# Loading 28 of the gathered edge chunks row by row from two other engines in a graph attention kernel

## The chip, the cores and the metric

The kernel runs on one core of a Trainium2 chip. The metric is the device time of one execution in microseconds (us); lower is better. TensorE is PE in the profile, VectorE DVE, ScalarE ACT, GpSimd POOL, SyncE SP. "SPq" and "ACTq" are records of an engine's instruction queue, such as the issue of a DMA.

## What is computed

One layer of graph attention with 4 heads of 32 over 12,500 nodes and 200,000 edges sorted by target, added to its input. Cut to what matters:

```
h = relu(layernorm(x))                         # node features, 128 wide
hn = (h @ W_node.T).reshape(N, 4, 32)
e = (edge_features @ W_edge.T).reshape(E, 4, 32)
att = sum(concat([hn[src], hn[tgt], e]) * a)   # one logit per edge and head
att = where(att > 0, att, 0.2 * att)
m = maximum(segment_max(att, tgt), 0)
ex = exp(att - m[tgt])
denom = segment_sum(ex, tgt) + (E - deg) * exp(-m)
out = x + segment_sum(ex / denom[tgt] * hn[src], tgt)
```

`hn[src]` reads one row of a node table per edge: a random read of 200,000 rows.

## The kernel before

A first part (about 90 us) normalizes the nodes and writes `table` to DRAM: one row of 137 floats (548 bytes) per node, with the projected features and the source part of the logits. Edges stand in groups of 512 places (511 edges and a first place that takes over a sum from the group before); a group has J = 4 chunks of 128, one edge per partition. QG = 4 groups are a quad; there are nq = 98 quads, q = 0 to 97. Supers are mostly 4 quads (near the ends 2 or 3); the softmax runs once per super.

For each quad `gather(q, ...)` issues 16 indirect DMAs on GpSimd (L183), one per chunk; each fetches 128 rows of `table` by the indices in `srci` into `ga`, a ring of QUADS = 8 quads. `open_logits(q)` orders the gathers of quad q + 2, so that GpSimd works through the quads in order, and a ring place must be free of the quad eight before it.

`all_logits(q)` makes the logits of a quad on TensorE (L686, L689) from edge features `ea`, one-hot target matrices `at` (VectorE, L656, from `db`), and target weights `pw`; SyncE loads these. In the next quad's logits `add_sources(q)` lets ScalarE wait until all 16 gathers of the quad have landed, and copies the source logits out of `ga` into `U` (L733). This copy is called U(q) below. At a super's end `softmax` goes through ScalarE, VectorE and TensorE in turn (on ScalarE low L795, low L800, fac L857, stack L869, xs L887).

`sums(q)` runs about five quads behind: per group, VectorE weighs the gathered rows (L1067 or L1026) and makes a one-hot matrix (L1069 or L1009), TensorE sums (L1100). Up to quad 74 several groups share one accumulation; from quad 75 on each group is its own, and between two groups ScalarE copies a carried row into the next group (ga L919) and a finished sum out (pt L979), with a TensorE product (L911) between the two; at a quad's end ScalarE makes `den` (L985). Each of the four steps of `sums(q)` is interleaved with a step of the logits of a later quad; instructions of one engine run in the order written.

`db_all` holds two tiles of target places of 4 x 512 integers for each partition; from quad 10 on only a quarter of each is used (bytes instead of integers).

Of the kernel before, what the change touches and what calls it, by code (L numbers as in the profile page):

```python
# [9 lines left out]
F32 = mybir.dt.float32  # L10
# [4 lines left out]
OP = mybir.AluOpType  # L15
AX = mybir.AxisListType

P = 128
# [8 lines left out]
R_CNT, R_SRC, ROW = H * HW, H * HW + 1, H * HW + 5  # L27

J = 4
GE = J * P  # L30
NE = GE - 1
WIDE, NARROW = 112, 80
QG = 4
# [13 lines left out]
SQUARE = 32  # L47
TWO = 2
HELD = 3
SETS = max(NODE_T, QG * J)  # L50
PAD = 1 << 20


def blocks(total, step):
    return [(i, min(step, total - i)) for i in range(0, total, step)]
# [14 lines left out]
def kernel(  # L70
# [39 lines left out]
    nc = tc.nc  # L110
    NT = -(-(N + P) // P)
    NP = NT * P
# [8 lines left out]
    table = dram.tile([NP, ROW], F32, name="table")  # L121
# [33 lines left out]
    quads = blocks(G, QG)  # L155
    nq = len(quads)
    first_fold = nq - FOLDS
# [6 lines left out]

    spare = consts.tile([P, 6 * SBG * H], F32, name="spare")
    ga_all = consts.tile([P, QUADS, QG, J, ROW], F32, name="ga")
    GA, GATHERED = {}, set()
    arrived = [tc.alloc_semaphore(f"rows{k}") for k in range(QUADS)]
    landings = {}

    def gather(q, rows, width, lo, hi):

        g0, m = quads[q]
        ga = GA[q] = ga_all[:, q % QUADS]
        chunks = lambda i: -(-min(E - (g0 + i) * NE + 1, GE) // P)
        for i in range(lo, hi):
            if chunks(i) < J:
                nc.vector.memset(ga[:, i, chunks(i):, :], 0.0)
        order = [(i, j) for i in range(lo, hi) for j in range(chunks(i))]
        if q >= 2 * QUADS:  # L180
            order.sort(key=lambda at: at != (hi - 1, 0))
        for i, j in order:
            came = nc.gpsimd.indirect_dma_start(  # L183
                out=ga[:, i, j, 0:width], out_offset=None, in_=rows,
                in_offset=bass.IndirectOffsetOnAxis(ap=srci[:, g0 + i, j:j + 1], axis=0))
            if q >= QUADS:
                came.then_inc(arrived[q % len(arrived)], 16)
                tc.no_tile_sem_insts.add(came.ins.name)
                tc.add_to_no_dep_group(f"rows{q}", came.ins)
                landings[q] = landings.get(q, 0) + 16  # L190
# [27 lines left out]
    with tc.manual_schedule():  # L218
# [4 lines left out]
        for m in sorted({m for _, m in supers}):  # L223
            for p in range(-(-m // 2)):
                n = min(2, m - 2 * p) * QG
                to = of_head[m, p] = consts.tile([PAIR * KH, H * m * QG], F32, name=f"of_head{m}_{p}")
# [17 lines left out]
        for _ in range(AT_ONCE):  # L244
            q, i = early.pop(0)
# [129 lines left out]
        db_all = stay.tile([P, 2, QG, GE], I32, name="db")  # L375
# [20 lines left out]
        with tc.tile_pool(name="node", bufs=2) as node, tc.tile_pool(  # L396
# [117 lines left out]
            for b, (t0, T) in enumerate(sets):  # L514
# [5 lines left out]
                row = node.tile([P, NODE_T, ROW], F32, name="row")  # L520
# [24 lines left out]
    with tc.tile_pool(name="work", bufs=2) as work, \  # L545
# [34 lines left out]
        def windows(of, size, w, n):  # L580
# [5 lines left out]
        as_bytes = lambda d: d.bitcast(U8)  # L586
        rows_at = lambda d, at, size, n: as_bytes(d.rearrange("n c -> (n c)"))[
            bass.ds(at, n * size)].rearrange("(n c) -> n c", c=size)
# [44 lines left out]
        def fetch_rows(s):  # L633
            g0, m = groups(s)
            dr = DR[s] = turned.tile([SBG * H, NE + 2], I32, name="dr", bufs=2)
            if finer(s) > 1:
# [4 lines left out]
            nc.sync.dma_start(dr[0:H * m, :],  # L641
                              dst_rows[g0:g0 + m, :].unsqueeze(0).to_broadcast([H, m, NE + 2]))

        def open_logits(q):
            if q == supers[of_quad[q]][0]:
                fetch_rows(of_quad[q])
            if q + 2 < nq:
                fetch(q + 2)
            AT[q] = work.tile([P, QG, GE], BF16, name="at")
# [68 lines left out]
        def add_sources(q):  # L718

            s = of_quad[q]  # L720
            g0, m = quads[q]
            s0, sm = groups(s)
            keep_logits(q)
            if s not in U:
                U[s] = turned.tile([P, J, SBG * H], F32, name="U", bufs=2)
            f = finer(s)
            u = U[s][:, 0:J // f, 0:sm * H * f].rearrange("p c (h w) -> p w c h", h=H)[
                :, (g0 - s0) * f:(g0 - s0 + m) * f]
            if q >= QUADS:
                nc.scalar.wait_ge(arrived[q % len(arrived)],  # L730
                                  sum(landings[a] for a in range(QUADS, q + 1)
                                      if a % len(arrived) == q % len(arrived)))
            taken = nc.scalar.copy(u, GA[q][:, :m].rearrange("p g (f c) r -> p (g f) c r", f=f)[  # L733
                :, :, :, R_SRC:R_SRC + H])
            if q >= QUADS:
                tc.declare_no_dep(taken.ins, group=f"rows{q}",
                                  reason="a semaphore counts the gathers of this quad")
                tc.declare_fence(taken.ins, group=f"rows{q}")
            for kept in (EA, DB, PW, AT):
                del kept[q]  # L740
# [153 lines left out]
        state = {"step": 0}  # L894

        def complete(window=True, all_due=False):

            state["step"] += 1
            division = None
            if divisions and "hold" not in state and (  # L900
                    all_due or divisions[0][-1] is None or divisions[0][-1] + 2 <= state["step"]):
                division = divisions.pop(0)
            if begun and window:
                complete_window(*begun.pop())
            if division:
                divide(*division)
# [132 lines left out]
        def sums(q):  # L1039
# [8 lines left out]
            s = of_quad[q]  # L1048
# [3 lines left out]
            k, span = class_of(q)  # L1052
# [23 lines left out]
            for i in range(m):  # L1076
                g = g0 + i
                if first_fold - 4 <= q < first_fold - 4 + FOLDS:
                    shifts(q + 4, i)
                on_gpsimd = early and (q, i) > (first_fold - 2, QG - 2)  # L1080
                if (q, i) not in AHEAD:
                    weighed(nc.gpsimd if on_gpsimd else nc.vector, ga, i,
                            heads(XE[s] if on_gpsimd else ex)[:, :, :, g - s0])
                    if not early:
                        mark(q, i, hot)
                new = i % k == 0
                if not i and not later:
                    entered()
                    settled()
                if new:  # L1090
                    second = k == 2 and i > 0
                    if not second:
                        bank = ps.tile([P, 512], F32, name="acc", bufs=3)
                    acc = bank[0:1 + span, ROW:2 * ROW] if second else bank[0:1 + span, 0:ROW]
                    fc = fac if g == s0 else None
                if later and i == m - 1:
                    entered()
                least_j = 1 if k == 1 else 0
                for j in range(least_j, J)[::-1]:
                    nc.tensor.matmul(acc, hot[:, i, j, 0:1 + span], ga[:, i, j, :],  # L1100
                                     start=new and j == J - 1 and not second,
                                     stop=k > 1 and i % k == k - 1 and j == least_j,
                                     skip_group_check=k > 1)
                if i == (2 if later else 1):
                    passed_on(fac if g0 == s0 else None)
                    if later:
                        settled()
                if not later and i == (2 if k > 1 else 1):
                    entered()
                    if k == 1:  # L1110
                        settled()
                complete(new)
                if k == 1:
                    begun.append((q, i, ga, hot, pt, acc, fc))
                if i == 2 and QUADS <= q < first_fold - 5 and of_quad[q + 1] == s:
                    READY[q + 1] = marks(q + 1)
                    beside_rows(q + 1)
                    RESTED.add(q + 1)
                if k > 1 and i == m - 1:
                    state["pending"] = q, bank  # L1120
                if QUADS <= q < first_fold - 5:
                    if i % TWO == 0 and (q, i + 1) not in AHEAD and i + 1 < m:
                        weighed(nc.vector, ga, i + 1, heads(ex)[:, :, :, g + 1 - s0])
                        mark(q, i + 1, hot)
                        AHEAD.add((q, i + 1))
                    elif i % TWO and i + 1 < m:
                        ready(q, i + 1, ga, hot)
                    elif i + 1 == m and q + 1 in READY:
                        ready(q + 1, 0, GA[q + 1], READY[q + 1])
                issue("inputs", "results")  # L1130
                yield
# [417 lines left out]
        with tc.manual_schedule():  # L1549
# [20 lines left out]
            for s, (q0, m) in enumerate(supers):  # L1570
# [17 lines left out]
                for k in range(m if s == 1 else m - 1):  # L1588
                    now, ahead = ahead[:1], ahead[1:]
                    several_sums = [sums(q0 + k)]  # L1590
                    if s == len(supers) - 3:
                        held_sums = sums(q0 + k + 1)
                        several_sums.append(islice(held_sums, HELD))
                    early_marks = (marked(first_fold - 2, first_fold - 1)
# [235 lines left out]
```

## Time and profile before

| | |
|---|---|
| median of 3 runs | 1998.37 us (1998.31 to 1999.74) |
| the profiled execution | 2000.29 us, span 1998.4 us |
| PE busy | 57% |
| DVE busy | 60% |
| ACT busy | 16% |
| POOL busy | 75% |
| mean granted TensorE clock | 0.732 |

The time of the profiled execution is 1.9 us above its span. In the lists, a group of instructions has its line, engine, operation, output and inputs, count, then busy time and mean ns of one, then the idle time of the engine just before and what ended it. A row of the timeline has start, duration, engine, line, operation, count, and in brackets the idle time before it. A row of waits has who waited for what, us in total, times, and the longest. Issuing a DMA is not counted as busy time of its engine.

### The profile page before, as it was taken

The numbers are of one execution on the slowest core, as the hardware profiler recorded it, in microseconds if no ns is written. First come the engines' busy times: TensorE is split into PE (matmuls) and PEld (weight loads), VectorE is DVE, ScalarE is ACT, GpSimd is POOL, SyncE is SP. The second block draws the span as 40 slices with busy tenths as digits, with TensorE's granted clock in tenths as the row PEclk, the third lists the DMA queues.
The fourth block names the chain that finished last, engine by engine and source line by source line (L and its number), as shares of the span: only waits on it lengthen the run. The fifth ranks groups of instructions, "written<-read, shape, count | busy, mean of one in ns | idle before, by whom it ended". The sixth has DMA issues, their size and how long they took to land. (4 is left out here: it accounts for less than half of the span.)

```text
span 1998.4 us, 18710 instructions
## 1 busy us (share of the span) xinstructions
PE 1145.4 (57%) x5116; PEld 779.1 (39%) x5116; DVE 1195.9 (60%) x2695; ACT 320.7 (16%) x1077; POOL 1496.4 (75%) x1596
## 2 busy tenths in 40 slices
PE   6566676555464555564646555646464554465565
PEld 5444354334243333343434333434343333234344
DVE  8676787456365554563755646637556465468585
ACT  6564111001001010010010100100101011122122
POOL 7777777777777777777777777777777777777775
PEclk9788788677676776766767767667677677777777
DMA  7754754434344434444444444444443453445441
GB/s 253 208 134 99 174 135 115 101 97 112 95 111 101 119 98 109 101 109 111 115 104 120 98 116 103 110 111 116 103 117 94 106 123 95 123 98 123 101 98 42
DMA packets 167746, 229.56 MB, mean 115 GB/s; under 512 B 60827, under 2 KB 100669, under 8 KB 167638
## 3 DMA queue, kind: packets, MB, share of 16 engines
q0 software_dynamic: 50112, 109.61, 24.9%
q1 hardware_dynamic: 115824, 116.14, 20.3%
q10 hardware_dynamic: 1702, 2.59, 0.4%
q8 instruction: 41, 0.67, 0.1%
q14 instruction: 67, 0.55, 0.1%
HBM read 210.74 MB, written 17.43 MB: 114 GB/s over the span
## 5 line engine op out<-in xcount | busy, mean ns | idle before, releaser
L183 POOL DMA_INDIRECT ga<-table,srci x1494 | 1413.2, 946 | 456.6 <-issue 427.1
L1100 PE MATMUL acc<-ga,hot 128*113 128x137 f32 (+1 forms) x2928 | 544.7, 346 | 95.3 <-DVE hot L1009 55.2
L1100 PEld LDWEIGHTS acc<-ga,hot 128*113 128x113 f32 (+1 forms) x2928 | 484.5, 215 | 193.4 <-issue 80.2
L947 DVE SCALAR_TENSOR_TENSOR pt<-pt,spare,acc 1x133 f32<-1x133 f32 x113 | 38.3, 339 | 517.9 <-ACT den_of L941 516.5
L689 PE MATMUL lg<-at,pw 112*96 112x512 bf16 (+2 forms) x392 | 156.4, 435 | 271.7 <-DVE at L656 257.5
L686 PE MATMUL lg<-ea,by_pair 128*96 128x512 f32 (+1 forms) x392 | 230.8, 674 | 11.4 <-ACT tg L699 11.4
L656 DVE TENSOR_TENSOR at<-const_ps,db 112x1024 bf16<-112x1024 f32 (+1 forms) x176 | 212.7, 1209 | 5.0 <-DMA db<-offset 4.1
L1067 DVE TENSOR_TENSOR ga<-ga,ex_ps 128x1056 f32<-128x1056 f32 x147 | 182.3, 1240 | 0.0
L790 PE MATMUL t_ps<-ident,U 128*64 128x128 f32 (+2 forms) x210 | 46.6, 393 | 196.5 <-ACT U L733 196.5
L733 ACT COPY U<-ga 128x64 f32<-128x64 f32 x98 | 29.0, 298 | 756.4 <-DMA ga<-table,srci 756.1
L1069 DVE TENSOR_TENSOR hot<-const_ps,slot 128x896 f32<-128x896 f32 (+1 forms) x147 | 144.2, 981 | 0.0
L881 PE MATMUL ex_ps<-ident,stack 128*128 128x128 f32 x105 | 28.8, 427 | 188.8 <-DVE stack L871 176.2
L790 PEld LDWEIGHTS t_ps<-ident,U 128*64 128x64 f32 (+2 forms) x210 | 37.1, 200 | 221.7 <-ACT U L733 216.1
L881 PEld LDWEIGHTS ex_ps<-ident,stack 128*128 128x128 f32 x105 | 18.6, 215 | 202.9 <-ACT stack L869 202.9
L689 PEld LDWEIGHTS <-pw 112*96 112x96 bf16 (+2 forms) x392 | 54.4, 139 | 104.4 <-issue 101.9
L966 PEld LDWEIGHTS acc<-pt,spare 1*2 1x2 f32 x226 | 14.0, 86 | 207.9 <-issue 199.6
L183 POOL DMA_INDIRECT ga<-in_x_dram,srci x72 | 68.3, 949 | 23.3 <-issue 18.9
L1026 DVE TENSOR_TENSOR ga<-ga,ex_ps 128x528 f32<-128x528 f32 x92 | 63.5, 693 | 36.5 <-ACT xs L887 36.5
L699 ACT COPY tg<-lg 96x512 f32<-96x512 f32 (+1 forms) x51 | 29.6, 580 | 291.9 <-PE lg L689 275.0
L715 PE MATMUL t_ps<-tg,of_head 96*64 96x512 f32 (+3 forms) x96 | 71.0, 831 | 3.4 <-ACT tg L699 3.4
L715 PEld LDWEIGHTS t_ps<-tg,of_head 96*64 96x64 f32 (+3 forms) x96 | 11.8, 170 | 153.0 <-issue 146.8
L686 PEld LDWEIGHTS lg<-ea,by_pair 128*96 128x96 f32 (+1 forms) x392 | 63.7, 188 | 18.2 <-ACT tg L699 13.8
(205 smaller groups left out, 1314.0 us busy)
## 6 DMA issues: line engine op xcount, KB each, us to landing
ea<-in_edge_t_dram SPq DMA_DIRECT2D x196, 256.0 KB
ga<-table,srci POOLq DMA_INDIRECT x1494
db<-offset SPq DMA_DIRECT2D x53, 256.0 KB
db<-in_dst_dram SPq DMA_DIRECT2D x20, 320.0 KB
db<-offset SPq DMA_DIRECT2D x35, 160.0 KB
table<-row SPq DMA_DIRECT2D x9, 616.5 KB
xt<-in_x_dram SPq DMA_DIRECT2D x9, 576.0 KB
inputs<-in_x_dram SPq DMA_DIRECT2D x92, 56.0 KB
```

What stands on the lines that cost most here:

```text
L183: came = nc.gpsimd.indirect_dma_start(out=ga[:, i, j, 0:width], out_offset=None, in_=rows, in_offset=bass.IndirectOffsetOnAxis(ap=srci[:, ...
L656: nc.vector.tensor_tensor(AT[q][:span, i:i + n, :].rearrange("p g e -> p (g e)"), part_ps[:span].to_broadcast([span, n * GE]), DB[q][:span ...
L686: nc.tensor.matmul(lg, by_pair[:, begin:begin + n], ea[:, i // 2, :], start=half == 0 and i == 0, stop=False, skip_group_check=True)
L689: nc.tensor.matmul(lg, PW[q][:span, begin:begin + n], at[:span, i, :], start=False, stop=full and i == quads[q][1] - 1, skip_group_check=True)
L715: nc.tensor.matmul(TP[s][:groups(s)[1] * H], of_head[supers[s][1], p][:n], tg[:n], start=p == 0, stop=False, skip_group_check=True)
L790: nc.tensor.matmul(t_ps[:R, j * P:(j + 1) * P], u[:, j, :R], ident, start=False, stop=j == C - 1, skip_group_check=True)
L881: nc.tensor.transpose(turned_ps[:, j, :], stack[:, j * P:(j + 1) * P], ident)
L947: nc.vector.scalar_tensor_tensor(to, row(w + at), passing[:, w + at:w + at + 1], own, op0=OP.mult, op1=OP.add)
L1026: engine.tensor_tensor(val, val, weight.unsqueeze(3).to_broadcast([P, J, H, HW]), op=OP.mult)
L1067: nc.vector.tensor_tensor(val, val, weight.unsqueeze(3).to_broadcast([P, TWO * J, H, HW]), op=OP.mult)
L1069: nc.vector.tensor_tensor(hot[:, i:i + TWO, :, 1:1 + span].rearrange("p g j c -> p (g j) c"), lane_ps[:, 0:span].unsqueeze(1).to_broadcast ...
L1100: nc.tensor.matmul(acc, hot[:, i, j, 0:1 + span], ga[:, i, j, :], start=new and j == J - 1 and not second, stop=k > 1 and i % k == k - 1 a ...
```

## The change

28 chunks are no longer gathered on GpSimd. In each of the four steps of `sums(q)`, for q = 12 to 91, ScalarE issues 7 loads of one table row each and SyncE 5, into tiles of their own in the unused part of `db_all` (two tiles for each of the engines). 19 steps of ScalarE fill one chunk (16 chunks in all, each the last chunk of a quad's last group), 26 steps of SyncE another (12 chunks, the chunk before that). The row addresses come from the index list: a DMA fetches 128 indices onto one partition, VectorE multiplies them by the row's bytes, and every fourth step the engine loads 28 (or 20) of them into registers. Each row counts on a semaphore; before U(q) ScalarE waits for the 128 rows of the chunk and copies them into the ring.

```
 SINGLES_FROM = 12
...
-        order = [(i, j) for i in range(lo, hi) for j in range(chunks(i))]
+        order = [(i, j) for i in range(lo, hi) for j in range(chunks(i)) if (q, i, j) not in SINGLE]
...
+        class Singles:
+            def __init__(self, engine, kind, some, j, at):
+                self.engine, self.kind, self.some, self.j = engine, kind, some, j
+                free = db_all.rearrange("p k g e -> p k (g e)")[:, :, GE * (1 + at):GE * (2 + at)]
+                self.rows = [free[:, k, 0:ROW].bitcast(F32) for k in range(2)]
+                self.places = [free[0:1, k, 2 * P:3 * P] for k in range(2)]
+                self.semaphores = [nc.alloc_semaphore(f"single{at}_{k}") for k in range(3)]
+                self.steps = -(-P // some)
+                self.step, self.first, self.count = 0, None, {}
+            def target(self, n):
+                return self.first + n * self.steps // QG
+            def chunk(self, n):
+                return self.target(n), QG - 1, self.j
+            def fetch_places(self, n):
...
+                self.engine.dma_start(self.places[n % 2], src[at:at + P].unsqueeze(0))
+            def scale_places(self, n):
+                if self.target(n) < nq - 2:
+                    nc.vector.tensor_scalar(self.places[n % 2], self.places[n % 2], float(4 * ROW),
+                                            None, op0=OP.mult)
+            def advance(self):
+                if self.first is None:
+                    self.first = state["opened"] + -(-self.steps // QG) + 1
+                    self.fetch_places(0)
+                    self.scale_places(0)
+                n, at = divmod(self.step, self.steps)
+                self.step += 1
+                q, i, j = self.chunk(n)
+                if q >= nq - 2:
+                    return
+                if not at:
+                    SINGLE[q, i, j] = self, n
+                    self.fetch_places(n + 1)
+                if at == QG // 2:
+                    self.scale_places(n + 1)
+                lo = at * self.some
+                if at % QG == 0:
+                    upto = min(lo + QG * self.some, P)
+                    self.values = nc.values_load_multi_w_load_instructions(
+                        self.places[n % 2][:, lo:upto], engines=[self.kind], ...)[1]
+                for p in range(lo, min(lo + self.some, P)):
+                    came = self.engine.dma_start(
+                        as_bytes(self.rows[n % 2][p:p + 1, :]),
+                        rows_at(table, self.values[p - at // QG * QG * self.some], 4 * ROW, 1))
+                    came.then_inc(self.semaphores[n % 3], 16)
...
+            def put(self, n, to):
+                nc.scalar.wait_ge(self.semaphores[n % 3], 16 * P * (n // 3 + 1))
+                taken = nc.scalar.copy(to, self.rows[n % 2])
...
+        SINGLES = [Singles(*of, at) for at, of in enumerate([(nc.scalar, mybir.EngineType.Activation, 7, 3), (nc.sync, mybir.EngineType.SP, 5, 2)])]
...
 def open_logits(q):
+            state["opened"] = q
...
 def add_sources(q):
+            for (a, i, j), (of, n) in list(SINGLE.items()):
+                if a == q:
+                    of.put(n, GA[q][:, i, j, :])
+                    del SINGLE[a, i, j]
...
 def sums(q):
                 complete(new)
+                if SINGLES_FROM <= q < first_fold - 5:
+                    for of in SINGLES:
+                        of.advance()
```

With first = opened + ceil(steps / 4) + 1 the n-th chunk of ScalarE belongs to quad 22 + 19n/4 (rounded down), that of SyncE to quad 24 + 26n/4. ScalarE's last rows are issued in `sums(87)`, SyncE's in `sums(89)`.

ScalarE, from U(84) to U(85), in the part where each group is its own accumulation. Before (U is L733, the carried row L919, the finished sum L979, the one-hot column and the softmax columns of the next quad L998 and L1037, den L985):

```order
L733 COPY U<-ga 128x4x16
L919 COPY ga<-acc 1x133
L979 COPY pt<-acc 81x137
L998 CAST hot<-is_last 128x16
L1037 COPY ga<-xs 128x16x5
L919 COPY ga<-acc 1x133
L979 COPY pt<-acc 81x137
L919 COPY ga<-acc 1x133
L979 COPY pt<-acc 81x137
L985 ACTIVATE den<-pt 81x16
```

After, the same beginning (lines are 80 higher; `DMA db<-table` are the row loads, `TENSOR_LOAD db` loads 28 addresses into registers):

```order
L813 COPY U<-ga 128x4x16
L999 COPY ga<-acc 1x133
L1059 COPY pt<-acc 81x137
L695 TENSOR_LOAD db
L700 DMA db<-table 1x548 x7
L1078 CAST hot<-is_last 128x16
L1117 COPY ga<-xs 128x16x5
L999 COPY ga<-acc 1x133
L1059 COPY pt<-acc 81x137
L700 DMA db<-table 1x548 x7
L999 COPY ga<-acc 1x133
L1059 COPY pt<-acc 81x137
```

Seven loads now stand behind each finished sum, ahead of the next carried row.

ScalarE in a softmax quad, from U(86). Before:

```order
L733 COPY U<-ga 128x4x16
L919 COPY ga<-acc 1x133
L979 COPY pt<-acc 81x137
L795 ACTIVATE low<-t_ps 64x511
L919 COPY ga<-acc 1x133
L979 COPY pt<-acc 81x137
L800 COPY low<-t_ps 64x511
L919 COPY ga<-acc 1x133
L979 COPY pt<-acc 81x137
L857 ACTIVATE fac<-fac 1x4
```

After:

```order
L700 DMA db<-table 1x548 x7
L875 ACTIVATE low<-t_ps 64x511
L999 COPY ga<-acc 1x133
L1059 COPY pt<-acc 81x137
L695 TENSOR_LOAD db
L700 DMA db<-table 1x548 x7
L880 COPY low<-t_ps 64x511
L999 COPY ga<-acc 1x133
L1059 COPY pt<-acc 81x137
L700 DMA db<-table 1x548 x7
L937 ACTIVATE fac<-fac 1x4
```

A block of loads stands ahead of each of the first three softmax steps. Two more blocks follow behind den of that quad (L985 before, L1065 now), ahead of the next U.

SyncE, a quad of the middle part (out: results; inputs: rows of x for the sum; ea, db, pw: for the logits). Before:

```order
L596 DMA out_dram<-res 112x512
L596 DMA ea<-in_edge_t_dram 128x512
L596 DMA out_dram<-res 112x512
L582 TENSOR_LOAD base_row
L596 DMA inputs<-in_x_dram 112x512
L582 TENSOR_LOAD base_side
L596 DMA inputs<-in_x_dram 112x512
L596 DMA pw<-side 112x24
```

After:

```order
L597 DMA out_dram<-res 112x512
L597 DMA ea<-in_edge_t_dram 128x512
L700 DMA db<-table 1x548 x5
L597 DMA out_dram<-res 112x512
L583 TENSOR_LOAD base_row
L700 DMA db<-table 1x548 x5
L597 DMA inputs<-in_x_dram 112x512
L583 TENSOR_LOAD base_side
L700 DMA db<-table 1x548 x5
L597 DMA inputs<-in_x_dram 112x512
L597 DMA pw<-side 112x24
```

Five loads stand between SyncE's other transfers, four times a quad.

More of the change, by code (lines that the diff above doesn't have):

```diff
@@ L49 @@
 HELD = 3
+SINGLES_FROM = 12
 SETS = max(NODE_T, QG * J)
@@ L166 @@
     ga_all = consts.tile([P, QUADS, QG, J, ROW], F32, name="ga")
-    GA, GATHERED = {}, set()
+    GA, GATHERED, SINGLE = {}, set(), {}
     arrived = [tc.alloc_semaphore(f"rows{k}") for k in range(QUADS)]
@@ L642, in fetch_rows @@
                               dst_rows[g0:g0 + m, :].unsqueeze(0).to_broadcast([H, m, NE + 2]))
+        class Singles:
[15 more added lines that the diff above has]
+                    return
+                g = quads[q][0] + i
+                at = ((g // 2 * J + j) * 2 + g % 2) * P
+                self.engine.dma_start(self.places[n % 2], src[at:at + P].unsqueeze(0))
[10 more added lines that the diff above has]
+                self.step += 1
+                q, i, j = self.chunk(n)
+                if q >= nq - 2:
+                    return
+                if not at:
+                    assert q not in GATHERED
+                    SINGLE[q, i, j] = self, n
[6 more added lines that the diff above has]
+                    self.values = nc.values_load_multi_w_load_instructions(
+                        self.places[n % 2][:, lo:upto], engines=[self.kind], min_val=0,
+                        max_val=(NP - 1) * 4 * ROW,
+                        skip_runtime_bounds_check_because="a node's row")[1]
+                for p in range(lo, min(lo + self.some, P)):
[3 more added lines that the diff above has]
+                    came.then_inc(self.semaphores[n % 3], 16)
+                    tc.no_tile_sem_insts.add(came.ins.name)
+                    tc.add_to_no_dep_group(f"single{self.j}_{n}", came.ins)
+                    self.count[n] = self.count.get(n, 0) + 1
+            def put(self, n, to):
+                assert self.count[n] == P
+                nc.scalar.wait_ge(self.semaphores[n % 3], 16 * P * (n // 3 + 1))
+                taken = nc.scalar.copy(to, self.rows[n % 2])
+                tc.declare_no_dep(taken.ins, group=f"single{self.j}_{n}",
+                                  reason="a semaphore counts the rows of this chunk")
+                tc.declare_fence(taken.ins, group=f"single{self.j}_{n}")
```

## The prediction

> **What bounds the kernel now.** I read the page's engine table and groups first, then the waits, then ScalarE's timeline.
>
> ```profile
> PE 1145.4 (57%) x5116; PEld 779.1 (39%) x5116; DVE 1195.9 (60%) x2695; ACT 320.7 (16%) x1077; POOL 1496.4 (75%) x1596
> L183 POOL DMA_INDIRECT ga<-table,srci x1494 | 1413.2, 946 | 456.6 <-issue 427.1
> ```
>
> GpSimd is the busiest engine, and its idle time is almost all "issue": it waits for nothing between two gathers.
>
> ```profile
> ACT U L733 <- DMA ga<-table,srci: 756.1, 73, 19.4
> POOL ga L183 <- issue: 446.0, 1463, 0.6
> ```
>
> In the list of waits the gather line has 1463 pauses of 0.3 us mean (446.0/1463) and none over 0.6, so GpSimd never stops for anyone; ScalarE stands 756 us at the copy U, which needs the quad's gathered rows. I write U(q) for the copy of quad q, and count them back from the last, q = 97. ScalarE's timeline shows where that wait has room:
>
> ```profile
> 1006.14 0.30 ACT L733 COPY U<-ga 128x64 f32<-128x64 f32 x1 [19.34 <-DMA ga<-table,srci]
> 1026.13 0.30 ACT L733 COPY U<-ga 128x64 f32<-128x64 f32 x1 [11.34 <-DMA ga<-table,srci]
> 1046.13 0.30 ACT L733 COPY U<-ga 128x64 f32<-128x64 f32 x1 [0.90 <-DMA ga<-table,srci]
> 1066.03 0.30 ACT L733 COPY U<-ga 128x64 f32<-128x64 f32 x1 [9.01 <-DMA ga<-table,srci]
> 1086.03 0.30 ACT L733 COPY U<-ga 128x64 f32<-128x64 f32 x1 [19.35 <-DMA ga<-table,srci]
> ...
> 1585.64 0.30 ACT L733 COPY U<-ga 128x64 f32<-128x64 f32 x1 [11.63 <-DMA ga<-table,srci]
> 1613.74 0.30 ACT L733 COPY U<-ga 128x64 f32<-128x64 f32 x1
> ...
> 1706.49 0.30 ACT L733 COPY U<-ga 128x64 f32<-128x64 f32 x1 [7.45 <-DMA ga<-table,srci]
> ...
> 1745.45 0.30 ACT L733 COPY U<-ga 128x64 f32<-128x64 f32 x1 [12.35 <-DMA ga<-table,srci]
> 1770.55 0.30 ACT L733 COPY U<-ga 128x64 f32<-128x64 f32 x1
> 1786.30 0.30 ACT L733 COPY U<-ga 128x64 f32<-128x64 f32 x1 [6.44 <-DMA ga<-table,srci]
> 1805.40 0.30 ACT L733 COPY U<-ga 128x64 f32<-128x64 f32 x1
> 1829.08 0.30 ACT L733 COPY U<-ga 128x64 f32<-128x64 f32 x1
> 1845.82 0.30 ACT L733 COPY U<-ga 128x64 f32<-128x64 f32 x1 [8.35 <-DMA ga<-table,srci]
> 1866.18 0.30 ACT L733 COPY U<-ga 128x64 f32<-128x64 f32 x1 [10.42 <-DMA ga<-table,srci]
> ...
> 1966.10 0.30 ACT L733 COPY U<-ga 128x64 f32<-128x64 f32 x1 [0.99 <-DMA ga<-table,srci]
> ```
>
> Three stretches. Up to about 1590 us U stands every 20 us: 79.89 us for 64 gathers, 1.248 us each, and some 40 us of each 80 are waiting (11.34, 0.90, 9.01, 19.35). The 0.90 ends the quad in which the softmax runs. Behind it (accumulations of one group each, quads from 75) the consumers need more: the softmax quad runs 25.1 us (1745.45 to 1770.55) and is caught up by the next ones. From U(92) at 1866.18 to the end, 132.2 us, the consumers run at their own pace; the last gather costs 0.99 us. So a gather saved before U(92) is worth its 1.248 us if the consumers are still ahead there.
>
> **What it removes.** 28 gathers: 28 x 1.248 = 34.9 us of GpSimd. By the rule of targets (first 22 + 4.75n for ScalarE, 24 + 6.5n for SyncE) 26 of them lie at or before quad 92: 32.4 us at U(92). Rows and bytes loaded are the same, so I cost the transfers themselves at nothing. The copy out of a singles' tile waits on ScalarE for its 128 rows, with U and all of ScalarE behind it; the last of them is issued one to two quads before, so that wait should be over when it is reached.
>
> **What it adds: the price of one row.** 16 chunks x 128 on ScalarE, 12 x 128 on SyncE, each a DMA of its own.
>
> ```profile
> 1804.39 0.25 ACTq L1148 DMA_DIRECT2D rows<-in_fine_ends_dram  x1
> 1804.69 0.58 ACT L699 COPY tg<-lg 48x512 f32<-48x512 f32 x1
> ...
> L596 SPq MOVE inputs<-in_x_dram x203: 29/29/38, 132.3 to 1953.7; - x102
> L596 SPq DMA_DIRECT2D inputs<-in_x_dram x203: 317/327/640, 132.3 to 1953.8; - x102
> ...
> L582 SPq TENSOR_LOAD <-base_side x98: 262/485/1366, 93.9 to 1906.6; - x98
> ...
> 1.18 0.45 ACTq L264 DMA_DIRECT2D we<-in_w_edge_dram  x1
> 1.66 0.45 ACTq L266 DMA_DIRECT2D ab<-in_a_cols_dram  x1
> ...
> PE ws_ps L271 <- DMA ab<-in_a_cols_dram: 5.1, 1, 5.1
> ```
>
> ScalarE's own issue of a one-partition load took 0.25 us, and the copy behind it began only 0.30 us after the issue did: an issue holds ScalarE's queue. With the MOVE that an address from a register needs (0.03) a row is 0.33 us. Below, 0.28 (no gap); above, 0.41 (SyncE's 0.327 for 80 to 112 partitions, plus MOVE and gap) and, with both queues issuing as at the start, 0.45 + 0.08 = 0.53. I take 0.33, since one partition is nearest to the first row.
>
> The Trainium skill speaks against the change: in DMA: Bandwidth & Descriptors, Rules for kernel authors, it says of many small transfers to coalesce them, since "under 64 KB you're paying mostly overhead", and gives about 2 us fixed per DMA. By it 28 rows would cost 56 us a quad if they queued for it; the rows above put ScalarE's second issue 0.48 us behind its first while the data of ab came 3.4 us after its issue, so here the latency overlaps and only the issue counts.
>
> Per quad, ScalarE gets 28 x 0.33 = 9.2, a register load 0.5 (the median above) and 0.1 for 28 copies of some 0.3 us over 80 quads: 9.9 us, in blocks of seven rows, 2.3 us. SyncE gets 20 x 0.33 + 0.5 = 7.1 us.
>
> ```profile
> SPq L596 <- DVE res L1312: 878.7, 72, 16.6
> ```
>
> SyncE waits 12.2 us a time for VectorE's results (878.7/72), more than 7.1, so I cost its part at nothing; queued behind it are the features, weights and targets of quads ahead. VectorE's 28 scalings of 128 addresses (some 0.2 us each) and their waits for the address load lie two steps behind the fetch: nothing in the first stretch, one or two instances in the second.
>
> **First stretch.** The ordinary quads have 9 to 19 us of wait for 9.9 us. In the softmax quad the blocks stand ahead of the three steps that wait anyway:
>
> ```profile
> 1028.48 0.59 ACT L795 ACTIVATE low<-t_ps 64x511 f32<-64x511 f32 x1 [2.06 <-PE t_ps L790]
> ...
> 1033.14 0.58 ACT L800 COPY low<-t_ps 64x511 f32<-64x511 f32 x1 [4.00 <-DVE t_ps L798]
> ...
> 1039.34 0.20 ACT L857 ACTIVATE fac<-fac 1x4 f32<-1x4 f32 x1 [5.62 <-DVE fac L856]
> ```
>
> 2.06, 4.00 and 5.62 us cover three blocks nearly; two more before the next U make it some 5 us late, and the next quad's 9 us take that up. GpSimd's ring is then far from full. The full 1.248 us per gather is won.
>
> **Second stretch.** Here ScalarE's copies lie on the path between the windows:
>
> ```profile
> 1712.42 0.27 ACT L979 COPY pt<-acc 81x137 f32<-81x137 f32 x1 [3.92 <-PE acc L911]
> 1713.57 0.27 ACT L979 COPY pt<-acc 81x137 f32<-81x137 f32 x1 [0.73 <-PE acc L911]
> 1714.79 0.27 ACT L979 COPY pt<-acc 81x137 f32<-81x137 f32 x1 [0.55 <-PE acc L911]
> ...
> 1749.85 0.27 ACT L979 COPY pt<-acc 81x137 f32<-81x137 f32 x1 [3.98 <-PE acc L911]
> ...
> 1753.06 0.27 ACT L979 COPY pt<-acc 81x137 f32<-81x137 f32 x1 [2.30 <-PE acc L911]
> ...
> 1759.61 0.20 ACT L857 ACTIVATE fac<-fac 1x4 f32<-1x4 f32 x1 [4.26 <-DVE fac L856]
> ```
>
> An ordinary quad takes ScalarE 8.6 us (1706.49 to 1715.06); the 3.92 covers the first block with its register load (2.8), the other three are added: 8.6 + 9.9 - 2.8 = 15.7 us. In the softmax quad five blocks stand: one ahead of low (2.3), one with a register load ahead of the second low (2.8, of which the 2.30 covers 1.3), one ahead of fac (covered by 4.26), two behind den (4.6): 25.1 + 8.4 = 33.5 us. The gathers of a quad now come every 19.5 us. The lag of U behind its gather, from zero at U(78) (1585.64, where ScalarE waited):
> - to U(82): 28.1 + 5 + 3 x 15.7 = 80.2 against 78.0: 2 us late
> - to U(86): 33.5 + 47.1 = 80.6 against 78.0: 5 late
> - to U(89), three quads: 33.5, 15.7, and the quad from 1786.30 (19.1 us, six blocks of which its long waits cover two: 29): 78.2 against 58.5: 24.5 late
> - to U(92), ScalarE's rows ending at sums(87): 23.7 + 8.4, then 8.4 + 5 (16.7 less its wait of 8.35, two blocks), then 9.9 (20.4 less 10.42): 55.4 against 58.5: 21 late.
>
> At U(92) the kernel is 32.4 - 21 = 11 us early, and the 0.99 at the last gather goes: **12 us**. The profiled execution took 2000.29 (span 1998.4 and 1.9 around it), the runs 1998.37; against the runs I forecast 1986.
>
> Each 0.01 us on a row moves the lag by about 2.8 us (some 40 uncovered blocks of 7). At 0.28 the lag is 21 - 14 = 7 and the time 1998.4 - 26 = 1972; with none at all, 1998.4 - 34 = 1964; at 0.41 it is 21 + 22 = 43: 2009.
>
> **Rivals.**
> - All of it hidden: 1964. For it, ScalarE is busy 16% of the span, and 756 us of its waits are for the gathers; against it, those waits are scarce just in the second stretch (five of the eight U above from 1745.45 on have waits, 38.6 us together).
> - ScalarE's issues become the bound of the second stretch. Break-even is 21 + 13 = 34 us of lag, a row of 0.375 us; at 0.41 it ends at 2009, at 0.53 at 2040. For it, 0.45 us issues when both queues issue together; against it, those loads have 128 partitions.
> - Address loads late: VectorE waits for the place row of each chunk. 28 waits of 3.4 us (ab above) are 95 us, nearly all in the first stretch, where 40 us per 80 are free; two in the second make 1993.
> - Each row holds its queue until it lands, as the small-transfer rule would have it: 28 x 3.4 = 95 us a quad, beyond 7000 us. The 0.48 us between two issues speaks against it.
> - The change does nothing since gathers did not bind: GpSimd's row of waits excludes that in the first stretch.
>
> **How the numbers follow.** Part of the gain lost, 1972 to 1994, my forecast: 0.40. All hidden, 1964 to 1972: 0.22. Address loads late, about 1993: 0.06. ScalarE bound, 1994 to 2010: 0.18, half of it within 0.2% (4 us, about what a measurement of this kernel can tell from no change); over 2010: 0.12; rows held until landing: 0.02. Range 1964 to 2010, which leaves out 0.14 above and a little below. Faster: 0.40 + 0.22 + 0.06 = 0.68; same 0.09; slower 0.23.
>
> **What would show it.** 1466 gathers from the table, still 1.248 us apart. ScalarE's row loads 0.25 to 0.33 us each with 0.08 between starts. U every 19.5 us up to 1550 us with waits left; from U(79) on U without waits, and the softmax quads 33 us. I am wrong if a row costs over 0.37, if blocks that I put on the path run beside it (then U still waits for gathers at 1700 us), or if GpSimd shows pauses over 1 us.

## The result, and the profile after

The changed kernel took 2001.03 us (median of 20 runs, 1999.38 to 2002.99), the kernel before beside it 1998.77 (20 runs): a ratio of 1.0013, 95% interval 1.0007 to 1.0019. It is 2.3 us slower, little but clear of the noise; the forecast was 1986, some 12 us faster. Four of the experiments below ran on one chip and four on another, on which the kernel before takes 2507 and 2513 us; all the others ran on chips where it takes 1998.

The page of the changed kernel: the engine table, then the gathers (count, busy us, mean ns of one, idle before).

```profile
PE 1156.8 (58%) x5116; PEld 787.2 (39%) x5116; DVE 1200.5 (60%) x2723; ACT 337.7 (17%) x1105; POOL 1469.9 (74%) x1568
L184 POOL DMA_INDIRECT ga<-table,srci x1466 | 1386.4, 946 | 447.2 <-issue 424.7
```

28 gathers are gone, and GpSimd still waits for nobody between two of them. The list of waits (total us, times, longest):

```profile
POOL ga L184 <- issue: 443.3, 1453, 0.3
ACT U L813 <- DMA ga<-table,srci: 424.6, 43, 18.5
```

The first row has no pause over 0.3 us, so the saving arrives on GpSimd. The timelines of GpSimd show it at the end, the last gather before and then after:

```profile
1962.13 0.95 POOL L183 DMA_INDIRECT ga<-table,srci  x1 [0.30 <-issue]
```

```profile
1926.11 0.94 POOL L184 DMA_INDIRECT ga<-table,srci  x1 [0.31 <-issue]
```

It comes 36.0 us earlier. The second row of waits says who did not follow: ScalarE waits for gathers at 43 quads in place of 73. Its timeline after, at the copies U from U(78) on:

```profile
1558.83 0.30 ACT L813 COPY U<-ga 128x64 f32<-128x64 f32 x1 [10.80 <-DMA ga<-table,srci]
1589.50 0.30 ACT L813 COPY U<-ga 128x64 f32<-128x64 f32 x1
...
1641.45 0.30 ACT L813 COPY U<-ga 128x64 f32<-128x64 f32 x1
1675.23 0.30 ACT L813 COPY U<-ga 128x64 f32<-128x64 f32 x1
1692.62 0.30 ACT L813 COPY U<-ga 128x64 f32<-128x64 f32 x1
1712.68 0.30 ACT L813 COPY U<-ga 128x64 f32<-128x64 f32 x1 [2.17 <-issue]
1727.03 0.30 ACT L813 COPY U<-ga 128x64 f32<-128x64 f32 x1
...
1810.85 0.30 ACT L813 COPY U<-ga 128x64 f32<-128x64 f32 x1
...
1867.23 0.30 ACT L813 COPY U<-ga 128x64 f32<-128x64 f32 x1
```

U(78) comes at 1558.83, 26.8 us earlier than before (1585.64): 21 gathers of the singles up to there are 26.2 us. It still waits 10.80 us for its gathers. From U(79) on no U does, and U(92) at 1867.23 is 1.0 us later than before. The whole gain of the first stretch is given back in these 308 us, and from U(92) to the end both kernels take 132.2 us.

Where it goes, one quad on ScalarE's timeline (ACTq rows are issues, x7 is a block of seven rows):

```profile
1697.51 0.27 ACT L1059 COPY pt<-acc 81x137 f32<-81x137 f32 x1 [4.48 <-PE acc L991]
1699.53 2.42 ACTq L700 DMA_DIRECT2D db<-table  x7
1702.00 0.22 ACT L1078 CAST hot<-is_last 128x16 f32<-128x16 bf16 x1 [4.21 <-issue]
1702.11 0.32 ACT L1117 COPY ga<-xs 128x80 f32<-128x80 f32 x1
1702.33 0.26 ACT L999 COPY ga<-acc 1x133 f32<-1x133 f32 x1
1703.14 0.27 ACT L1059 COPY pt<-acc 81x137 f32<-81x137 f32 x1 [0.55 <-PE acc L991]
1703.21 2.20 ACTq L700 DMA_DIRECT2D db<-table  x7
1705.45 0.26 ACT L999 COPY ga<-acc 1x133 f32<-1x133 f32 x1 [2.04 <-issue]
```

Each block stands between two copies that TensorE's next window needs. A block is 2.20 us. But at 1697.78 something else comes first: 1.75 us in which ScalarE neither copies nor issues a row. That is the register load of 28 addresses, which its queue starts while the copy still runs (at 1697.5, for 1.88 us). All of its kind by line (min, median and max in ns, first and last start):

```profile
L695 SPq TENSOR_LOAD <-db x84: 527/1300/1472, 337.0 to 1882.3; - x84
L695 ACTq TENSOR_LOAD <-db x80: 1179/1948/2123, 336.9 to 1843.8; - x80
```

```profile
L700 ACTq DMA_DIRECT2D db<-table x2048: 227/235/659, 339.0 to 1852.4; - x187
```

A register load of 28 takes 1.95 us (the median; the last one of a chunk has 16 and takes 1.18), where the prediction had put 0.5. A row's issue takes 0.235.

### The profile page after: what moved, and what is told of

Same layout as the page of the kernel before. It is cut to its first block, busy times and chain, and to the rows that moved or that the text cites. A ratio compares the mean times of both kernels' runs of the same rounds, so it can differ in the third digit from the quotient of the medians.

```text
span 1999.4 us, 26161 instructions
## 1 busy us (share of the span) xinstructions
PE 1156.8 (58%) x5116; PEld 787.2 (39%) x5116; DVE 1200.5 (60%) x2723; ACT 337.7 (17%) x1105; POOL 1469.9 (74%) x1568
## 4 chain that ended last, share of the span: by engine, by line
POOL 33%; DVE 21%; issue 15%; PE 12%; ACTq 7%; ACT 6%; DMA 5%; SPq 0%; POOLq 0%; DVEq 0%
POOL ga L184 33%; ACTq L700 6%; DMA ga<-table,srci 4%; PE acc L1180 3%; PE acc L991 2%; PE lg L762 2%; PE t_ps L870 1%; DVE at L732 1%; DVE t_ps L944 1%; ACTq L695 1%; DVE t_ps L941 1%; DVE ga L1106 1%; DVE t_ps L884 1%; DVE t_ps L883 1%; DVE stats L288 1%
## 5 line engine op out<-in xcount | busy, mean ns | idle before, releaser
L184 POOL DMA_INDIRECT ga<-table,srci x1466 | 1386.4, 946 | 447.2 <-issue 424.7
L1180 PE MATMUL acc<-ga,hot 128*113 128x137 f32 (+1 forms) x2928 | 546.8, 347 | 73.4 <-DVE hot L1089 54.5
L1180 PEld LDWEIGHTS acc<-ga,hot 128*113 128x113 f32 (+1 forms) x2928 | 490.0, 216 | 165.3 <-issue 79.3
L762 PE MATMUL lg<-ea,by_pair 128*96 128x512 f32 (+1 forms) x392 | 245.9, 714 | 73.3 <-ACT tg L775 73.3
L991 PE MATMUL acc<-ga,hot 128*81 128x137 f32 x176 | 49.2, 371 | 71.6 <-ACT ga L999 66.1
L791 PE MATMUL t_ps<-tg,of_head 96*64 96x512 f32 (+3 forms) x96 | 61.9, 732 | 23.0 <-ACT tg L775 23.0
```

What stands on the lines that cost most here:

```text
L184: came = nc.gpsimd.indirect_dma_start(out=ga[:, i, j, 0:width], out_offset=None, in_=rows, in_offset=bass.IndirectOffsetOnAxis(ap=srci[:, ...
L762: nc.tensor.matmul(lg, by_pair[:, begin:begin + n], ea[:, i // 2, :], start=half == 0 and i == 0, stop=False, skip_group_check=True)
L791: nc.tensor.matmul(TP[s][:groups(s)[1] * H], of_head[supers[s][1], p][:n], tg[:n], start=p == 0, stop=False, skip_group_check=True)
L991: nc.tensor.matmul(acc, hot[:, i, 0, 0:acc.shape[0]], ga[:, i, 0, :], start=False, stop=stop)
```

## The experiments

Theory A: ScalarE's queue is the loss; rows and register loads in the second stretch delay the copies between windows. Theory B: SyncE's rows make its loads late. Theory C: thousands of one-row transfers slow everything a little. Theory D, formed after the first runs: each added instruction costs by itself.

**Rows only in the first stretch (e1, f1).** Both engines stop after `sums(74)`, with 13 + 9 chunks:

```
-    if q >= nq - 2:
+    if q >= nq - 2 or n >= self.most:      # most = (75 - 12) * 4 // steps
```

> Row loads only in sums(12) to sums(74), that is before each group has its own accumulation: 13 chunks on ScalarE and 9 on SyncE. Theory A (ScalarE's queue in the second stretch, 0.33 us a row and 1.95 us a register load on the path between the windows, gives the saving back): 22 x 1.248 = 27.5 us are kept, about 1971 us. Theory B (SyncE's rows make its other transfers late in the second stretch): also about 1971. Theory C (the one-row transfers slow gathers and other transfers wherever they run): most of the loss stays, 1990 or more.

**One engine alone (e2 and f2: ScalarE, 16 chunks; e3 and f3: SyncE, 12).** The list `SINGLES` keeps one of its entries:

```
-[(nc.scalar, ...Activation, 7, 3), (nc.sync, ...SP, 5, 2)]
+[(nc.scalar, ...Activation, 7, 3)]        # e2, f2
+[(nc.sync, ...SP, 5, 2)]                  # e3, f3
```

> ScalarE's 16 chunks alone, through sums(91); SyncE loads no rows. A: 15 chunks at or before quad 92 save 18.7 us there, and ScalarE's queue still makes the second stretch some 30 us late: about 2010 us, slower than before. B: nothing is late, 1998.8 - 18.7 = 1980. C: between, with half the rows, about 1990 to 2000.

> SyncE's 12 chunks alone, through sums(91); ScalarE loads no rows and copies 12 chunks into the ring. A: 11 chunks at or before quad 92 save 13.7 us and nothing is given back: about 1985. B: the second stretch is as late as with both: about 2015. C: about 1990 to 2000.

**One register load (e4, f4).** Every engine loads addresses once and uses them for all its chunks:

```
-    if at % QG == 0:
+    if at % QG == 0 and not hasattr(self, "values"):
```

> All 28 chunks, but each engine loads addresses into registers only once, at the first step, and uses these addresses for every chunk; the later register loads are left out, so wrong rows are fetched. A: 12 to 13 register loads of 1.95 us on ScalarE's path between U(79) and U(91) go, 20 to 25 us: about 1978. B and C: ScalarE's loads are not the cause, about 2000.

The four ran on a chip where the kernel before takes 2506.69: e1 2707.88 (ratio 1.0786, 1.0764 to 1.0809), e2 2712.05 (1.0791, 1.0745 to 1.0837), e3 2605.74 (1.0382, 1.0345 to 1.0418), e4 2737.58 (1.0931, 1.0908 to 1.0955). All were much slower, against every theory. The waits of e1:

```profile
POOL ga L184 <- issue: 758.6, 1474, 17.7
DVE at L733 <- DMA db<-offset: 521.4, 35, 28.5
PEld L766 <- issue: 389.9, 281, 22.4
```

GpSimd, free of everybody elsewhere, pauses up to 17.7 us with nothing to wait for that the profile shows, and so does TensorE's weight load (the third row); VectorE waits for target places, 521 us in all. That suggested theory D: e1 has 24562 instructions, 5852 more than the kernel before, for 201 us, 0.034 us each; e3 0.031, e4 0.032, e2 0.048. The same four kernels went to another chip:

> The same kernel as e1_first_stretch (22 chunks, rows only in sums(12) to sums(74)), to be read on a chip on which the kernel before takes about 1999 us. A (ScalarE's queue in the second stretch gives the saving back): 27 us less than before, about 1971. B (SyncE's rows make its other transfers late in the second stretch): the same. C (the one-row transfers slow others wherever they run): 1990 or more. D, new from the runs where the kernel before took 2507 us: every added instruction costs the engines fetch time, about 0.03 us each over all: 5,850 more instructions, slower than before here too.

> ScalarE's 16 chunks alone, as e2_scalar_only. A: about 2010, slower than before. B: 1980. C: 1990 to 2000. D: more than 100 us slower.

> SyncE's 12 chunks alone, as e3_sync_only. A: 13.7 us saved, about 1985. B: about 2015. C: 1990 to 2000. D: about 100 us slower.

> All 28 chunks with one register load for each engine and wrong rows, as e4_registers_once. A: 20 to 25 us less than the changed kernel, about 1978. B and C: about 2000. D: more than 200 us slower than before.

| against 1998.15 | time, us | ratio, 95% interval |
|---|---|---|
| f1, first stretch only | 1972.49 | 0.9864 (0.9847 to 0.9880) |
| f2, ScalarE alone | 2009.04 | 1.0049 (1.0032 to 1.0066) |
| f3, SyncE alone | 1985.25 | 0.9934 (0.9918 to 0.9951) |
| f4, one register load | 1977.44 | 0.9892 (0.9876 to 0.9909) |

f1 still has 22 of the 28 chunks and 79% of the instructions added, and gains 26 us: C is refuted, and D too where the kernel before takes 1998 (5852 more instructions, 26 us less). At U(92) f1 waits for a gather, as the kernel before does, 27.3 us earlier; its register loads cost as much as those of the changed kernel and are hidden:

```profile
1838.86 0.30 ACT L814 COPY U<-ga 128x64 f32<-128x64 f32 x1 [9.20 <-DMA ga<-table,srci]
```

```profile
L696 ACTq TENSOR_LOAD <-db x65: 1195/1983/2128, 335.8 to 1525.5; - x65
```

f3 refutes B: SyncE's rows to the end give 13 us. The waits of f3 show why its lateness does not matter: VectorE waits more for target places (59.2 us, 4.1 in the kernel before), but ScalarE's waits for the gathers are almost what they were:

```profile
ACT U L813 <- DMA ga<-table,srci: 729.3, 74, 19.6
...
DVE at L732 <- DMA db<-offset: 59.2, 12, 9.4
```

f2, ScalarE alone, ends slower than before, so the loss is ScalarE's. f4 takes the register loads away and leaves the rows (it fetches the same few rows for every chunk, and in neither kernel does a copy out of the tiles wait for its rows in this stretch); from U(78) to U(92) it needs 284.2 us (1559.84 to 1844.06) for the changed kernel's 308.4, and its time is 23.6 us shorter:

```profile
L695 ACTq TENSOR_LOAD <-db x1: 1942/1942/1942, 339.1 to 339.1; - x1
```

The changed kernel has 13 of ScalarE's register loads there (1590 to 1870 us):

```profile
L695 ACTq TENSOR_LOAD <-db x13: 1179/1901/2003, 1594.7 to 1843.8; - x13
```

13 x 1.9 = 24.7 us, and the stretch is 24.2 us shorter without them: the register loads stood on the path with their whole time, within 1 us. f4 leaves out SyncE's register loads too; that these cost nothing here is read from f3, which has them.

**ScalarE to `sums(74)`, SyncE to the end (g1, h1); SyncE with 7 rows a step (g2).** From f1 and f3: each where it is hidden.

```
+SINGLES: (nc.scalar, ...Activation, 7, 3, until 75), (nc.sync, ...SP, 5, 2, until 92)   # g1, h1
+SINGLES: ...                                         (nc.sync, ...SP, 7, 2, until 92)   # g2
```

> ScalarE's rows only in sums(12) to sums(74) (13 chunks), SyncE's through sums(91) (12 chunks): 25 chunks. A (only ScalarE's queue in the second stretch costs): 24 chunks at or before quad 92 save 30.0 us: about 1968. If SyncE's rows make its transfers late in the second stretch (B in part): no better than with both ended at 75, 1972 or more.

> As g1_sync_to_the_end, with 7 rows a step on SyncE instead of 5: 13 + 16 chunks, 28 of them at or before quad 92. SyncE then issues some 9.2 us of rows and 1.95 of register load a quad beside 7 to 8 us of its own, against 19.5 us. A: 34 us saved, 1964. B: SyncE's own loads come late in the second stretch, the targets above all: over 1975.

**Rows in one go (g3, h3).** From quad 75 on, ScalarE's 28 rows of a quad in its last step, not 7 in each:

```
-    of.advance()
+    late = of is SINGLES[0] and class_of(q)[0] == 1
+    for _ in range(1 if not late else QG if i == QG - 1 else 0):
+        of.advance()
```

> All 28 chunks as in the changed kernel, but from quad 75 on ScalarE issues the 28 rows of a quad behind the third window's sum in one go, where 7 stood behind each. If what counts is that rows stand between two windows (each breaks the chain from ScalarE to TensorE and back), time falls: three of four blocks leave the path, to about 1980. If ScalarE's whole time in a quad counts (rows 9.2, register load 1.95, its own work and its waits for TensorE, which then cover no rows), an ordinary quad takes 8.6 + 11.2 = 19.8 us for 17.2: later by some 20 us, about 2020.

**Nine rows a step, early (g4, h4).** h1 with 9 rows a step on ScalarE and registers loaded every third step:

```
-    if at % QG == 0:
-        upto = min(lo + QG * self.some, P)
+    if at % 3 == 0:
+        upto = min(lo + 3 * self.some, P)
```

> As g1_sync_to_the_end, with 9 rows a step on ScalarE instead of 7 (27 addresses loaded every third step): 16 chunks in the first stretch and 12 on SyncE, 28 as in the changed kernel, 27 at or before quad 92. A: 27 x 1.248 = 33.7 us saved, about 1964, if ScalarE's 36 rows (11.9 us) and register loads (some 2.6) a quad still fit the first stretch (three ordinary quads of 16 us and a softmax quad of 27 against 78). If not, the consumers come late from quad 12 on: 1985 or more.

These fell on a chip where the kernel before takes 2513.22: g1 2742.18 (1.0921, 1.0891 to 1.0951), g2 2939.07 (1.1703, 1.1669 to 1.1737), g3 2829.54 (1.1273, 1.1238 to 1.1307), g4 2935.96 (1.1678, 1.1639 to 1.1716). They decide nothing on A, and g2 was not run elsewhere. The others were:

> The kernel of g1_sync_to_the_end (13 chunks on ScalarE up to sums(74), 12 on SyncE up to sums(91)), to be read where the kernel before takes about 1999 us. A (only ScalarE's queue in the second stretch costs): 24 chunks at or before quad 92 save 30.0 us, about 1968. B in part (SyncE's rows make its own loads late in the second stretch; with SyncE alone VectorE waited 59 us for targets, in 12 instances): 1972 or more. Where the kernel before takes 2510 us: 9% slower again.

> The kernel of g3_rows_in_one_go (28 chunks; from quad 75 on ScalarE's 28 rows of a quad behind the third window's sum in one go). If only the place between two windows counts: about 1980. If ScalarE's whole time in a quad counts: about 2020, later than the changed kernel by some 20 us.

> The kernel of g4_nine_rows_early (16 chunks on ScalarE with 9 rows a step up to sums(74), 12 on SyncE up to sums(91)). A: 33.7 us saved, about 1964, if the first stretch still holds 36 rows a quad on ScalarE; 1985 or more if not.

Against 1998.20: h1 1967.95 (0.9849, 0.9836 to 0.9863), as expected. h3 took 2030.40 (1.0165, 1.0150 to 1.0181), 29 us above the changed kernel: the loss is not that rows stand between two windows, since with fewer such places it grows. As the expectation has it, ScalarE's whole time counts, and blocks of seven ran in part in its waits for TensorE's sums, which one block of a quad does not: from U(78) to U(92) these waits are 115 us in h3 and 81 in the changed kernel. That h3 came out 10 us above the expected 2020 is not traced further. Its timeline (the block of 28 holds a register load too):

```profile
1708.59 0.27 ACT L1059 COPY pt<-acc 81x137 f32<-81x137 f32 x1 [2.41 <-PE acc L991]
1708.66 11.37 ACTq L700 DMA_DIRECT2D db<-table  x28
1720.07 0.26 ACT L999 COPY ga<-acc 1x133 f32<-1x133 f32 x1 [11.21 <-issue]
```

h4 was a miss: 2029.37 (1.0156, 1.0142 to 1.0170), where more rows in the first stretch should have gained or done little. Its register loads by line, and then single ones of SyncE's and ScalarE's over one chunk:

```profile
L696 SPq TENSOR_LOAD <-db x108: 539/3080/3398, 336.0 to 1912.4; - x108
L696 ACTq TENSOR_LOAD <-db x80: 1443/5992/6278, 335.9 to 1556.7; - x80
...
L696 SPq TENSOR_LOAD <-db x1: 1594/1594/1594, 468.7 to 468.7; - x1
L696 SPq TENSOR_LOAD <-db x1: 3091/3091/3091, 484.0 to 484.0; - x1
...
L696 SPq TENSOR_LOAD <-db x1: 1593/1593/1593, 532.1 to 532.1; - x1
L696 SPq TENSOR_LOAD <-db x1: 3088/3088/3088, 545.2 to 545.2; - x1
...
L696 ACTq TENSOR_LOAD <-db x1: 2458/2458/2458, 495.7 to 495.7; - x1
L696 ACTq TENSOR_LOAD <-db x1: 6120/6120/6120, 507.8 to 507.8; - x1
```

SyncE's loads of 15 addresses start at places 0, 15, 30, ... of the chunk. Those that start at 0 and at 60 take 1.59 us (468.7 and 532.1); those at 15, 30, 45 and 75 take 3.1 to 3.3. ScalarE's 27 take 2.46 from place 0 and 6.1 from 27. The same number of addresses, 15, takes 1.59 or 3.1 by where it starts (the expectation of i5 below puts it down to the count alone). So a load that starts at a multiple of four and has a multiple of four addresses costs about 0.07 us for each (28 in 1.95, 20 in 1.30, 8 in 0.53), from such a start another number 0.09 to 0.11 (27 in 2.46, 15 in 1.59), and from any other start 0.2.

The 61 us that h4 takes above h1 arise mostly in two places. U(78) comes at 1591.72 against 1560.12: 31.6 us are lost while ScalarE loads rows; up to 6 us a register load is more than a quad's waits hold. From U(78) to U(92) h4 takes 298.2 us against 276.8, though ScalarE loads nothing there. SyncE does, with 3.1 us for most of its loads: it waits for others only 4 us in this stretch, 36 in h1, and VectorE waits 83.7 us for target places, 43.3 in h1. So theory B, which f3 refutes for SyncE's loads of 1.3 us, seems to hold for these; no run tried them alone.

**Eight and ten rows a step (i5, i6).** h1 with loads of 16 and of 20 addresses, all at multiples of four, every second step:

```
-    if at % QG == 0:
+    if at % 2 == 0:      # ScalarE alone; 8 rows a step in i5, 10 in i6
```

> As h1_sync_to_the_end, with 8 rows a step on ScalarE instead of 7 up to sums(74), addresses loaded 16 at a time every second step: 15 + 12 chunks, 26 at or before quad 92. In the run with nine rows a load of 27 values took 5.99 us and one of 15 values 3.08, where 28 took 1.95, 20 took 1.30 and 16 some 1.18: 0.2 us a value unless the count is a multiple of four. If that, and not the rows, made it late: 8 x 4 x 0.33 + 2 x 1.18 = 12.9 us a quad on ScalarE, 26 x 1.248 = 32.4 saved, about 1966. If the first stretch has no room for more than 28 rows: 1980 or more.

> As i5_eight_rows with 10 rows a step, addresses loaded 20 at a time every second step: 19 + 12 chunks, 30 at or before quad 92. 40 x 0.33 + 2 x 1.3 = 15.8 us a quad on ScalarE, less than the 20 that the run with nine rows had: if the register loads made that late, 30 x 1.248 = 37.4 us saved, about 1961; if the first stretch has no room for 40 rows (softmax quad 19 + 12, three of 17.5, 83 us against 77.5 a super), 2000 or more.

Against 1998.26: i5 1966.90 (0.9840, 0.9827 to 0.9853), i6 1961.67 (0.9817, 0.9802 to 0.9832). i6, with 19 + 12 chunks, is the fastest version and beats both kernels. In its list of waits ScalarE's waits for gathers are 110.5 us where f1 has 505.4, so not much more should fit; that was not tried:

```profile
ACT U L815 <- issue: 209.8, 21, 13.8
...
ACT U L815 <- DMA ga<-table,srci: 110.5, 21, 13.5
```

## Why the prediction was wrong, step by step

- **28 x 1.248 us on GpSimd: right.** The last gather comes 36.0 us earlier.
- **The row, 0.33 us: right.** Seven take 2.19 to 2.20 from the first start to the last end, so (2.20 - 0.235)/6 = 0.327 from start to start. The rows alone, with one register load (f4), leave 21 us of the gain. The rule of the Trainium skill that the forecast weighed (DMA: Bandwidth & Descriptors, Rules for kernel authors), to coalesce small transfers, did not decide here: f3's 1536 loads of one row gain 13 us, since SyncE's queue had the time. The 2 us a DMA that the forecast gave beside this rule are the Trainium skill's figure for DMAs that GpSimd issues (the same page, Anatomy of one DMA). Here ScalarE and SyncE issue the rows, on ScalarE 0.327 us apart.
- **The first stretch, free: right.** U(78) is early by 26.8 us for 26.2 us of gathers; f1 gains 26 us. The register loads of 1.95 us were hidden there too.
- **SyncE at no cost: right.** h1, with SyncE's rows to `sums(89)`, is 4.5 us below f1. The rival of late address loads did not occur: in f3's list VectorE waits for them once, 3.0 us. With loads of 3.1 us SyncE's part seems no longer free (h4).
- **Second stretch: the term that failed is the register load, in its size and in what was to cover it.** The forecast put it at 0.5 us, and in ordinary quads at nothing: "the 3.92 covers the first block with its register load (2.8)". It took 1.95, and no wait covered it.

  The size was read from the median of SyncE's 98 loads (485 ns), and those load one, two or four addresses. The rows by count, which the prediction did not separate, are in the profile before: loads from `base_row` between 1000 and 1400 us, of two addresses, and between 1600 and 1900 us, of four:

```profile
L582 SPq TENSOR_LOAD <-base_row x20: 469/476/498, 1010.9 to 1390.3; - x20
...
L582 SPq TENSOR_LOAD <-base_row x16: 863/874/967, 1617.6 to 1895.6; - x16
```

  These rows give 0.2 us for each more: 28 would have been put at 5.6 us, far over the truth, but the range would have had to hold everything from 0.5 to 5.6. The Trainium skill gives a price of that size on Runtime: NRT & Kernel Launch, section Instruction fetch mechanics: some 200 ns a register "even for bulk", of loads from HBM. The rows above and h4's 3.09 us for 15 agree with it, here for loads from on-chip memory; the 1.95 us for 28 does not.

  The cover shows in ScalarE's waits for the finished sums between U(78) and U(92): first the kernel before, then f4 (rows without register loads), then the changed kernel:

```profile
ACT pt L979 <- PE acc L911: 99.4, 56, 5.1
```

```profile
ACT pt L1059 <- PE acc L991: 78.5, 55, 5.0
```

```profile
ACT pt L1059 <- PE acc L991: 76.0, 54, 5.3
```

  With a few more that the trace puts down to another line of TensorE (L1180: 0.7 us in f4, 5.3 in the changed kernel) they are 79 and 81 us. So the rows shorten them by some 20 us and the register loads by nothing; the idle time of ScalarE that ends with "issue" grows from 78 to 103 us, by the 25 us of the loads. An ordinary quad, forecast at 15.7 us, takes 15.9 in f4 and 17.3 in the changed kernel (means of the three behind U(79) and the three behind U(83)). With 1.95 us and the 3.92 as cover it would have been 8.6 + 11.3 - 3.9 = 16.0: the size alone does not give it.
- **The sum.** U(78) to U(92) was forecast at 294.4 us (80.2 + 80.6 + 78.2 + 55.4) and took 308.4. The 13 register loads have at most 13 x 0.5 = 6.5 us of that forecast, and took 24.2; the rest was put at 287.9 or more, and took 284.2 (f4). So the loads were some 18 us too low, and the rest, by luck in the other direction, some 4 too high. The lag at U(92) is so 14 us above the forecast, 35, and the break-even had been put at 34: the outcome is the rival "ScalarE's issues become the bound", reached by the register loads, not by the rows whose price that rival had varied. The signs that the prediction named for its own forecast (U without waits for gathers from U(79), softmax quads of 33 us) are there, 33.8 and 34.4 us for U(82) and U(86): they did not tell the forecast from this rival.

## What to carry to other kernels

When work moves from a bound engine to the queue of an idle one, price everything that this queue then does, per instruction kind and by its size, and sum it where that engine stands on the path; idle share says nothing there. Here the row loads of the first stretch, where ScalarE's waits are long, gain 26 us, and ScalarE's in the second, where they are short, lose all of it again: stop the edit at that border (f1, h1), and beyond it use a queue that has waits of its own left (SyncE's, as long as its register loads are short). A wait beside an added instruction is no cover by itself: TensorE's waits grew shorter by the rows and not by the register loads. A median over instructions of several sizes is no price for a size outside them.

## What the runs showed that was not expected

- A register load from on-chip memory goes by where it starts: 28 addresses from a multiple of four take 1.95 us, 27 from place 0 take 2.46 and from place 27 6.1. h4, which has such loads on both engines, is 61 us slower than h1.
- On two chips the kernel before takes 2507 and 2513 us, and each kernel with added instructions loses 99 us to 426 us more; there e1's engines pause with nothing to wait for that the profile shows. Divided by the instructions added, the loss is between 0.031 us (e3) and 0.057 us (g4), so theory D has no one price there. The rows of the first stretch, which gain 26 us in f1, lose 201 there. What differs in these chips was not tried and stays open.
